# Two token transposes of a graph-attention kernel: from TensorE to block-permuted loads and VectorE

## The chip, the cores and the metric

The kernel runs on one core of one Trainium2 chip. The metric is device time in microseconds, from the start to the end of one execution. Five engines run their own instruction streams in order and meet at semaphores: TensorE (PE, with its weight loads PEld), VectorE (DVE), ScalarE (ACT), GpSimd (POOL) and SyncE (SP), which here issues every DMA.

## The reference, cut to what matters

The input x has 128 graphs of 64 nodes and 768 features. Two layers follow each other, each of the form layernorm(x + layer(x)):

```python
# layer 0: 12 heads of 64, over the neighbours that adj allows
h    = x @ W                                  # 768 x 768
attn = softmax(mask(leaky(src(tanh(h)) + dst(tanh(h)).T)))
out  = elu(attn @ h + b)
gate = sigmoid(x @ H_w.T + H_b)
x1   = layernorm(x + gate * out + (1 - gate) * x)
# layer 1: 6 heads of 128
q, k, v = x1 @ Wq, x1 @ Wk, x1 @ Wv
ctx  = softmax(mask(q @ k.T / sqrt(128))) @ v
out  = layernorm(x1 + ctx @ Wf + bf)
```

All in float32. So each token tile is multiplied from the left four times: x by W and H_w, x1 by Wv (and by Wq and Wk in layer 1). TensorE contracts over partitions, so these products need the tile with its features, not its tokens, on the partitions: x and x1 have to be transposed.

## The kernel before, in words

Two graphs make a tile of 128 tokens by 768 features (64 tiles), and two tiles make a pair (`NP` = 32 pairs). `phase_a` does layer 0 and the v product of layer 1, pair by pair; `phase_b` does the rest of layer 1 in groups of two pairs. Every product of a pair (256 tokens by 768 by 768) is done in seven half-size block products in place of eight, in Strassen's manner: class `Product` takes sums of blocks of the transposed tokens (`token_sums`, four GpSimd additions per pair, L252 to L255) and of the weights, multiplies them (L203) and puts the results together from PSUM.

**The order is written by hand.** `phase_a` fills a dictionary `events` by step with `at(step, ...)`, and `run` emits the steps in turn. A pair starts `N` = 21 steps after the one before it. At its offset `o`, pair `p` runs block `i` of the product W at step `o + i`, of G (the gate) at `o + 7 + i`; the product V (v of layer 1) of pair `p` follows at `o + 56`, thus in the steps 14 to 20 of a later pair. One step is therefore one block, and 21 blocks make one period: W, G, V of three pairs that overlap. Within a step the closures are emitted in the order in which they were registered, and each engine gets its instructions in that order.

**What a block leaves behind.** `Product.evict(i)` is called after block `i`. Blocks 0, 2 and 3 are kept as snapshots in SBUF (`snap`, ACT, L381). Blocks 1, 4 and 5 are read from PSUM and added to a snapshot by VectorE (`into`, L404 for h and the gate; L423 for v). Block 6 adds onto the PSUM tile X that blocks 0, 2 and 4 wrote, and is copied out by ACT. Four PSUM tiles go round (`psX`).

**The transposes.** `transposed(src, chunk)` makes a tile T of 128 features by 6 chunks by 128 tokens: six PE transposes against the identity into two PSUM tiles (L375), copied to SBUF by ACT (L376). `xT` calls it for x of a pair's two tiles at steps `o - 6` and `o - 5`, and `sums` runs the four GpSimd sums at `o - 4`. For x, chunk `c` of each half of 384 features holds every third feature (`chunk0`, by which the rows of W and H_w are also ordered). For x1, chunks are 128 features in a row (`chunk1`); `x1T` transposes at `o + 42` and `o + 43`, writes the result to DRAM for layer 1 (`xT_d`), and `sums` follows at `o + 44`. T tiles come from a pool of four.

**Other work of a pair.** For each of its two tiles `Tile0` runs the attention in steps after `s` (`s = o` for tile 1, `s = o + 5` for tile 0): tanh, source and target scores (L444 to L454), the exchange through DRAM of target scores (`dst_out`, `dst_in`), the exchange of halves of h in SBUF (`exchange`, `hx`), GpSimd's addition (L492), the mask on VectorE (L499), maximum, subtraction and sum (L503, L504, L511), GpSimd's scaling (L514), the transposition of probabilities on PE (L525), the aggregation (L543), elu and the mix (L562 to L583), the layernorm, and the write of x1 to DRAM (`spill`, L594).

All DMAs go through SP's single queue, in program order; an issue that waits for an engine holds those behind it.

Of the kernel before, what the change touches and what calls it, by code (L numbers as in the profile page):

```python
# [9 lines left out]
F32 = mybir.dt.float32  # L10
# [5 lines left out]
P = 128  # L16
# [45 lines left out]
def kernel(  # L62
# [31 lines left out]
    nc = tc.nc  # L94
    NB, S, D = x.shape
# [3 lines left out]
    NC = D // P  # L99
    HALF = D // 2  # L100
    CH = NC // 2
    NT = NB * S // P
    NP = NT // 2
    assert S == 64 and DH == P and E == 64 and HALF == 384 and A == 12

    x_t = x.rearrange("(t g) n d -> t (g n) d", g=2)
# [11 lines left out]
    ident = const.tile([P, P], F32, name="ident")  # L118
# [32 lines left out]
    def load15(wb, src, k):  # L151

        kb, c = divmod(k, 2)
        nc.sync.dma_start(
            wb[:, 3 * kb : 3 * kb + 3, c, :],
            src[k * P : (k + 1) * P, :].rearrange("p (n o) -> p n o", n=3),
        )

    def weight15_sum(wb, k, eng):
        to, a, b, sign = WEIGHT_SUMS[k]  # L160
        eng.tensor_tensor(wb[:, to], wb[:, a], wb[:, b], SIGN[sign])
# [7 lines left out]
    def weight_plain(wb, src, blocks):  # L169
        for kh, oh in blocks:  # L170
                nc.sync.dma_start(
                    wb[:, SLOT[kh, oh]],
                    src[kh * HALF : (kh + 1) * HALF, oh * HALF : (oh + 1) * HALF].rearrange(
                        "(c p) o -> p c o", p=P
                    ),
                )

# [71 lines left out]
    def token_sums(Ss, Ta, Tb):  # L249

        tt = nc.gpsimd.tensor_tensor
        tt(Ss[:, 0], Tb[:, :CH], Tb[:, CH:], ALU.add)  # L252
        tt(Ss[:, 1], Ss[:, 0], Ta[:, :CH], ALU.subtract)
        tt(Ss[:, 2], Ta[:, :CH], Tb[:, :CH], ALU.subtract)
        tt(Ss[:, 3], Ta[:, CH:], Ss[:, 1], ALU.subtract)  # L255
# [44 lines left out]
    def phase_a(ctx):  # L300
        k6 = ctx.enter_context(tc.tile_pool(name="k6", bufs=2))
        k3 = ctx.enter_context(tc.tile_pool(name="k3", bufs=1))
        k1 = ctx.enter_context(tc.tile_pool(name="k1", bufs=1))
        small = ctx.enter_context(tc.tile_pool(name="small", bufs=3))
        psa = ctx.enter_context(tc.tile_pool(name="psa", bufs=4, space=bass.MemoryType.PSUM))

        st = [dict() for _ in range(NP)]
# [6 lines left out]
        def load(p):  # L314
            d = st[p]
            d["x"] = []
            for i in range(2):
                t = xb[:, (2 * p + i) % 7]
                nc.sync.dma_start(t, x_t[2 * p + i])
                d["x"].append(t)  # L320
            d["adj"] = small.tile([P, 2, S], U8, name="adj")
            nc.sync.dma_start(d["adj"], adj_p[p])
# [39 lines left out]
        def chunk0(src, k):  # L362
            return src.rearrange("p (h q c) -> p h c q", h=2, c=CH)[:, k // CH, k % CH, :]

        def chunk1(src, k):
            return src[:, k * P : (k + 1) * P]

        def transposed(src, chunk):

            dst = k3.tile([P, NC, P], F32, name="T", bufs=4)  # L370
            for half in range(2):
                ps = psa.tile([P, CH, P], F32, name="pa")
                for c in range(CH):
                    k = half * CH + c
                    nc.tensor.transpose(ps[:, c, :], chunk(src, k), ident)  # L375
                nc.scalar.copy(dst[:, half * CH : (half + 1) * CH, :], ps)  # L376
            return dst

# [5 lines left out]
        def sums(d):  # L384
            Ss = k6.tile([P, 4, CH, P], F32, name="S")
            token_sums(Ss, *d["T"])
            d["S"] = Ss
# [20 lines left out]
        def start_h(d):  # L408
            d["h"] = [k3.tile([P, D], F32, name="h", bufs=3) for _ in range(2)]
            d["W"] = product(d, lambda i, c: w0_v[:, i, :, c, :], into(d["h"]))  # L410

        def start_g(d):
            d["g"] = [k3.tile([P, D], F32, name="gt", bufs=3) for _ in range(2)]
            d["G"] = product(d, lambda i, c: w1[:, i, c, :], into(d["g"]))

        def start_v(d):
            def sink(k, ps, kept):
                i, half = PLACE[k]
                o = k1.tile([P, HALF], F32, name="v", bufs=3)
                if kept is None:  # L420
                    nc.scalar.copy(o, ps)
                else:
                    nc.vector.tensor_tensor(o, ps, kept, ALU.add)  # L423
                nc.sync.dma_start(v_d[2 * d["p"] + i][:, halves(half)], o)

            d["V"] = product(d, lambda i, c: w2[:, i, c, :], sink)
# [171 lines left out]
        def at(step, *fs):  # L598
            events.setdefault(max(step, 0), []).extend(fs)

        def dense(d, key, i):
            d[key].matmuls(i)
            d[key].evict(i)
# [11 lines left out]
        for k, block in enumerate(((0, 0), (1, 0), (0, 1), (1, 1))):  # L615
            at(10 + 5 * k, lambda block=block: weight_plain(w2, Wv, [block]))
# [4 lines left out]
        for p in range(NP):  # L621
            d, o = st[p], N * p
            d["p"] = p
            if p:
                at(max(o - 20, 1), lambda p=p: load(p))

            def xT(d, i):
                d.setdefault("T", []).append(transposed(d["x"][i], chunk0))

            at(o - 6, lambda d=d: xT(d, 0))  # L630
            at(o - 5, lambda d=d: xT(d, 1))
            at(o - 4, lambda d=d: sums(d))
            at(o, lambda d=d: start_h(d))
            at(o + 7, lambda d=d: start_g(d))
            for i in range(7):
                at(o + i, lambda d=d, i=i: dense(d, "W", i))
                at(o + 7 + i, lambda d=d, i=i: dense(d, "G", i))
            for i, s in ((1, o), (0, o + 5)):
                t = Tile0(p, i)
                at(s + 6 + (i == 0), t.tanh, t.cap)  # L640
                at(s + 7, t.src_mul)
                at(s + 8, t.src_sum, t.dst_mul)
                at(s + 9, t.dst_sum, t.dst_out, t.exchange)
                at(s + 13, t.dst_in)
                at(s + 14, t.gate)
                at(s + 17, t.add)
                at(s + 18, t.mask)
                at(s + 19, t.top)
                at(s + 20, t.total)
                at(s + 23, t.probs)  # L650
                at(s + 24, t.aggregate)
                at(s + 25, t.elu)
                at(s + 26, t.mix1)
                at(s + 27, t.mix2)
                at(s + 28, t.norm1)
                at(s + 29, t.norm2)
                at(s + 30, t.spill)

            def x1T(d, i):
                if i == 0:  # L660
                    d["T"] = []
                d["T"].append(transposed(d["x"][i], chunk1))
                nc.sync.dma_start(xT_d[d["p"]][:, i], d["T"][i])

            at(o + 42, lambda d=d: x1T(d, 0))
            at(o + 43, lambda d=d: x1T(d, 1))

            def reload_T(d):
                d["T"] = []
                for i in range(2):  # L670
                    t = k3.tile([P, NC, P], F32, name="T", bufs=4)
                    nc.sync.dma_start(t, xT_d[d["p"]][:, i])
                    d["T"].append(t)

            if p != NP - 4:
                at(o + 44, lambda d=d: sums(d))

            v = o + {NP - 4: 84, NP - 2: 50, NP - 1: 45}.get(p, 56)
            if p == NP - 4:
                at(v - 7, lambda d=d: reload_T(d))  # L680
                at(v - 3, lambda d=d: sums(d))
            at(v, lambda d=d: start_v(d))
            for i in range(7):
                at(v + i, lambda d=d, i=i: dense(d, "V", i))
# [24 lines left out]
    def phase_b(ctx, wq, wk):  # L709
# [269 lines left out]
        for k in range(NC):  # L979
            at(2 + k, lambda k=k: load15(wf, Wf, k))  # L980
# [120 lines left out]
```

## Time and profile before

Median of three runs: 3027.14 us (3026.11 to 3029.84). The profiled execution spans 3023.9 us at a granted TensorE clock of 0.993.

| engine | busy us | share | instructions |
|---|---|---|---|
| PE | 2935.8 | 97% | 18852 |
| PEld | 2139.9 | 71% | 18852 |
| DVE | 1798.6 | 59% | 3531 |
| ACT | 937.8 | 31% | 1743 |
| POOL | 1640.8 | 54% | 1648 |

The DMA queue of SP moved 257.16 MB; its packets took 25.7% of the time of 16 DMA engines. Layer 0 with v takes the first half of the span, up to about 1590 us.

How to read the profile: a group line gives line, engine, operation and shapes, how often, the busy time in all, the mean of one in ns, and the idle time just before it with what ended it. A timeline line gives the start, the length and the operation, with the idle time before it in brackets. The ends of matmuls are modelled, so for PE the distance between starts says more than the lengths. L numbers are those of the kernel before.

### The profile page before, as it was taken

The numbers are of one execution on the slowest core, as the hardware profiler recorded it, in microseconds if no ns is written. First come the engines' busy times: TensorE is split into PE (matmuls) and PEld (weight loads), VectorE is DVE, ScalarE is ACT, GpSimd is POOL, SyncE is SP. The second block draws the span as 40 slices with busy tenths as digits, with TensorE's granted clock in tenths as the row PEclk, the third lists the DMA queues.
The fourth block names the chain that finished last, engine by engine and source line by source line (L and its number), as shares of the span: only waits on it lengthen the run. The fifth ranks groups of instructions, "written<-read, shape, count | busy, mean of one in ns | idle before, by whom it ended". The sixth has DMA issues, their size and how long they took to land.

```text
span 3023.9 us, 49367 instructions
## 1 busy us (share of the span) xinstructions
PE 2935.8 (97%) x18852; PEld 2139.9 (71%) x18852; DVE 1798.6 (59%) x3531; ACT 937.8 (31%) x1743; POOL 1640.8 (54%) x1648
## 2 busy tenths in 40 slices
PE   7899999999999999999899999999999999999997
PEld 4566666666666666666557888888888888888886
DVE  4666666666676666766674555555555555555556
ACT  3343443434434444444422122222112222211221
POOL 3756565665656556565574444554544455454445
PEclk9999999999999999999999999999999999999999
DMA  5232232222322222232252121222112122211221
GB/s 158 67 98 92 89 110 77 98 87 93 105 82 98 82 98 98 84 103 82 87 173 80 49 85 60 78 85 82 57 63 85 59 80 85 81 57 64 85 79 69
DMA packets 224044, 260.31 MB, mean 86 GB/s; under 512 B 91713, under 2 KB 169281, under 8 KB 223809
## 3 DMA queue, kind: packets, MB, share of 16 engines
q1 hardware_dynamic: 223808, 257.16, 25.7%
q8 instruction: 150, 2.46, 0.3%
q14 instruction: 86, 0.70, 0.1%
HBM read 143.43 MB, written 101.06 MB: 81 GB/s over the span
## 4 chain that ended last, share of the span: by engine, by line
PE 66%; POOL 16%; DVE 12%; ACT 2%; issue 2%; DMA 1%; SPq 0%; DVEq 0%; POOLq 0%
PE X L796 29%; PE X L203 29%; POOL S L766 5%; POOL Sc L778 3%; PE pa L375 2%; DVE e L573 2%; POOL xs L754 2%; POOL tmp L444 2%; PE pb L921 2%; PE pb L861 2%; POOL rstd L290 2%; DVE e L574 1%; DVE e L582 1%; DVE st L278 1%; DVE h L404 1%
## 5 line engine op out<-in xcount | busy, mean ns | idle before, releaser
L203 PE MATMUL X<-w,S 128*128 128x384 f32 x2304 | 806.2, 493 | 15.3 <-ACT snap L381 8.3
L796 PE MATMUL X<-S,w 128*128 128x256 f32 x2816 | 669.7, 383 | 18.1 <-ACT q L817 14.8
L203 PEld LDWEIGHTS X<-w,S 128*128 128x128 f32 x2304 | 425.1, 191 | 315.2 <-ACT snap L381 28.1
L203 PE MATMUL X<-w,T 128*128 128x384 f32 x1728 | 608.2, 492 | 1.8 <-ACT T L376 1.0
L796 PEld LDWEIGHTS X<-S,w 128*128 128x128 f32 x2816 | 523.7, 190 | 96.6 <-issue 20.0
L203 PEld LDWEIGHTS X<-w,T 128*128 128x128 f32 x1728 | 320.8, 192 | 201.9 <-issue 4.2
L778 POOL TENSOR_TENSOR Sc<-cT 128x256 f32<-128x256 f32 x224 | 161.4, 730 | 378.6 <-PE X L796 375.0
L796 PE MATMUL X<-w,Sc 128*128 128x256 f32 x1408 | 326.9, 383 | 3.9 <-DVE xs L839 2.6
L839 DVE TENSOR_TENSOR xs<-xs,X 128x256 f32<-128x256 f32 x512 | 208.3, 418 | 179.3 <-PE X L796 147.8
L796 PEld LDWEIGHTS X<-w,Sc 128*128 128x128 f32 x1408 | 263.4, 190 | 47.1 <-DVE xs L839 10.4
L290 POOL TENSOR_TENSOR rstd<-rstd,neg_half 128x1 f32<-128x1 f32 x126 | 69.4, 551 | 398.9 <-DVE rstd L289 398.9
L822 DVE TENSOR_TENSOR k<-k,X 128x256 f32<-128x256 f32 x320 | 133.5, 421 | 218.3 <-PE X L796 168.3
L822 DVE TENSOR_TENSOR q<-q,X 128x256 f32<-128x256 f32 x320 | 131.9, 419 | 203.5 <-PE X L796 122.4
L796 PE MATMUL X<-xb,w 128*128 128x256 f32 x960 | 236.6, 379 | 0.0
L297 ACT ACTIVATE xs<-xs,shift,rstd 128x768 f32<-128x768 f32 x62 | 63.7, 1027 | 471.9 <-POOL shift L293 467.2
L796 PEld LDWEIGHTS X<-xb,w 128*128 128x128 f32 x960 | 181.2, 190 | 24.0
L817 ACT ACTIVATE k<-X,bk_c 128x256 f32<-128x256 f32 x192 | 91.0, 474 | 304.8 <-PE X L796 304.8
L895 POOL TENSOR_TENSOR s<-s,rs 128x384 f32<-128x384 f32 x64 | 53.1, 830 | 243.4 <-DVE rs L894 220.6
L766 POOL TENSOR_TENSOR S<-xb 128x512 f32<-128x512 f32 x104 | 131.6, 1279 | 84.2 <-DMA xb<-xT_d 56.7
L514 POOL TENSOR_TENSOR s<-s,rs 128x768 f32<-128x768 f32 x64 | 94.2, 1472 | 143.9 <-DVE rs L513 134.4
L817 ACT ACTIVATE q<-X,bq_c 128x256 f32<-128x256 f32 x192 | 89.0, 470 | 258.4 <-PE X L796 258.4
L381 ACT COPY snap<-X 128x384 f32<-128x384 f32 x288 | 136.5, 479 | 82.2 <-PE X L203 79.1
(106 smaller groups left out, 4262.8 us busy)
## 6 DMA issues: line engine op xcount, KB each, us to landing
xb<-in_x_dram SPq DMA_DIRECT2D x64, 384.0 KB
s<-dst_d SPq DMA_DIRECT2D x128, 192.0 KB
x_d<-xb SPq DMA_DIRECT2D x64, 384.0 KB
xT_d<-T SPq DMA_DIRECT2D x64, 384.0 KB
v_d<-v SPq DMA_DIRECT2D x128, 192.0 KB
xb<-xT_d SPq DMA_DIRECT2D x32, 768.0 KB
xb<-v_d SPq DMA_DIRECT2D x256, 96.0 KB
xs<-x_d SPq DMA_DIRECT2D x64, 384.0 KB
```

The source lines that it names most:

```text
L203: nc.tensor.matmul(o, self.lhsT(i, c), rhs, start=first and c == 0, stop=last and c == CH - 1, skip_group_check=True,)
L290: nc.gpsimd.tensor_tensor(rstd, rstd, neg_half, ALU.pow)
L297: nc.scalar.activation(r, r, AF.Identity, bias=shift, scale=rstd)
L375: nc.tensor.transpose(ps[:, c, :], chunk(src, k), ident)
L381: nc.scalar.copy(t, ps)
L514: nc.gpsimd.tensor_tensor(self.s, self.s, self.rs[:, :, None].to_broadcast([P, A, S]), ALU.mult)
L766: eng.tensor_tensor(t, group_part(d, r0), group_part(d, r1), op)
L778: nc.gpsimd.tensor_tensor(t, pair_part(d, q, r0), pair_part(d, q, r1), op)
L796: nc.tensor.matmul(ps, self.lhsT(r, slot, c), self.rhs(r, slot, c), start=start and c == 0, stop=stop and c == 1, skip_group_check=True,)
L817: nc.scalar.activation(o[:, b], ps, AF.Identity, bias=bias[:, hd : hd + 1], scale=1.0 if positive else -1.0)
L822: nc.vector.tensor_tensor(o[:, b], o[:, b], ps, ALU.add if positive else ALU.subtract)
L839: nc.vector.tensor_tensor(o, o, ps, ALU.add if positive else ALU.subtract)
```

## The change

x and x1 are no longer transposed by PE and copied by ACT. A second load brings the tile from DRAM with its 32x32 blocks already in transposed places (`load_blocks`: eight DMAs, each 32 partitions by 4 pieces of 96 floats), into a tile `xp` of which there is one. VectorE's `transpose`, which turns each 32x32 block in itself, then gives T (`turn`, two instructions a tile). x comes from the input a second time, x1 from where `spill` put it. The purpose is to take the transposes from PE and their copies from ACT.

The first pair's x and the last pair's x1 stay on PE (`transposed`, now without its `chunk` argument). x1 now has the same order of features as x, so Wq, Wk and Wv are loaded with their rows in that order (`in_order` and `"(p c) o -> p c o"`); Wf is not. In x1's case tile 1 is turned first. The pool `small` goes from three buffers to two, which makes room for `xp`.

```diff
     def load15(wb, src, k):
         kb, c = divmod(k, 2)
+        rows = src[k * P : (k + 1) * P, :] if src is Wf else in_order(src)[k]
...
-                        "(c p) o -> p c o", p=P
+                        "(p c) o -> p c o", p=P
...
-        small = ctx.enter_context(tc.tile_pool(name="small", bufs=3))
+        small = ctx.enter_context(tc.tile_pool(name="small", bufs=2))
...
+        def load_blocks(tile_, src):
+            xp = tile_.rearrange("p (h t r) -> p h t r", h=2, t=4)
+            sv = src.rearrange("(t i) (h q r) -> q h i t r", t=4, h=2, q=4)
+            for q in range(4):
+                for h in range(2):
+                    nc.sync.dma_start(xp[q * 32 : (q + 1) * 32, h], sv[q, h])
+            return xp
+
+        def turn(xp):
+            dst = k3.tile([P, NC, P], F32, name="T", bufs=4)
+            for h in range(2):
+                nc.vector.transpose(
+                    dst[:, h * CH : (h + 1) * CH, :].rearrange("p c (t i) -> p c t i", t=4),
+                    xp[:, h].rearrange("p t (j c) -> p c t j", c=CH),
+                )
+            return dst
+
+        def blocks(src):
+            return load_blocks(k3.tile([P, D], F32, name="xp"), src)
...
+            def xb_in(d, i):
+                d.setdefault("xp", []).append(blocks(x_t[2 * d["p"] + i]))
+
             def xT(d, i):
-                d.setdefault("T", []).append(transposed(d["x"][i], chunk0))
-
-            at(o - 6, lambda d=d: xT(d, 0))
-            at(o - 5, lambda d=d: xT(d, 1))
-            at(o - 4, lambda d=d: sums(d))
+                d.setdefault("T", []).append(turn(d["xp"][i]))
+
+            if p:
+                at(o - 12, lambda d=d: xb_in(d, 0))
+                at(o - 6, lambda d=d: xT(d, 0))
+                at(o - 6, lambda d=d: xb_in(d, 1))
+                at(o - 3, lambda d=d: xT(d, 1))
+            else:
+                at(0, lambda d=d: d.update(T=[transposed(t) for t in d["x"]]))
+            at(o - 2, lambda d=d: sums(d))
...
-            at(o + 42, lambda d=d: x1T(d, 0))
-            at(o + 43, lambda d=d: x1T(d, 1))
+            if p < NP - 1:
+                at(o + 40, lambda d=d: x1_in(d, 1))
+                at(o + 42, lambda d=d: x1T(d, 1, turn(d["xp", 1])))
+                at(o + 42, lambda d=d: x1_in(d, 0))
+                at(o + 45, lambda d=d: x1T(d, 0, turn(d["xp", 0])))
+            else:
+                for i in range(2):
+                    at(o + 42 + i, lambda d=d, i=i: x1T(d, i, transposed(d["x"][i])))
...
             if p != NP - 4:
-                at(o + 44, lambda d=d: sums(d))
+                at(o + (46 if p < NP - 1 else 44), lambda d=d: x1_sums(d))
```

More of the change, by code (lines that the diff above doesn't have):

```diff
@@ L153, in load15, with in_order @@
         kb, c = divmod(k, 2)
+        rows = src[k * P : (k + 1) * P, :] if src is Wf else in_order(src)[k]
         nc.sync.dma_start(
-            wb[:, 3 * kb : 3 * kb + 3, c, :],
-            src[k * P : (k + 1) * P, :].rearrange("p (n o) -> p n o", n=3),
-        )
+            wb[:, 3 * kb : 3 * kb + 3, c, :], rows.rearrange("p (n o) -> p n o", n=3)
+        )
+    def in_order(src):
+        r = src.rearrange("(h p c) o -> h c p o", h=2, c=CH)
+        return [r[k // CH, k % CH] for k in range(NC)]
     def weight15_sum(wb, k, eng):
@@ L363, in chunk0, with transposed @@
             return src.rearrange("p (h q c) -> p h c q", h=2, c=CH)[:, k // CH, k % CH, :]
-        def chunk1(src, k):
-            return src[:, k * P : (k + 1) * P]
-        def transposed(src, chunk):
+        def load_blocks(tile_, src):
[15 more added lines that the diff above has]
+            return load_blocks(k3.tile([P, D], F32, name="xp"), src)
+        def transposed(src):
             dst = k3.tile([P, NC, P], F32, name="T", bufs=4)
@@ L373, in transposed @@
                 for c in range(CH):
-                    k = half * CH + c
-                    nc.tensor.transpose(ps[:, c, :], chunk(src, k), ident)
+                    nc.tensor.transpose(ps[:, c, :], chunk0(src, half * CH + c), ident)
                 nc.scalar.copy(dst[:, half * CH : (half + 1) * CH, :], ps)
@@ L657, in phase_a, with x1_in, x1T @@
                 at(s + 30, t.spill)
[L659 to L663, printed above, removed]
-            at(o + 42, lambda d=d: x1T(d, 0))
-            at(o + 43, lambda d=d: x1T(d, 1))
+            def x1_in(d, i):
+                d["xp", i] = blocks(x1_d[2 * d["p"] + i])
+            def x1T(d, i, t):
+                d["x1T", i] = t
+                nc.sync.dma_start(xT_d[d["p"]][:, i], t)
+            if p < NP - 1:
[6 more added lines that the diff above has]
+                    at(o + 42 + i, lambda d=d, i=i: x1T(d, i, transposed(d["x"][i])))
             def reload_T(d):
@@ L673, in reload_T, with x1_sums @@
                     d["T"].append(t)
+            def x1_sums(d):
+                d["T"] = [d["x1T", i] for i in range(2)]
+                sums(d)
             if p != NP - 4:
-                at(o + 44, lambda d=d: sums(d))
+                at(o + (46 if p < NP - 1 else 44), lambda d=d: x1_sums(d))
             v = o + {NP - 4: 84, NP - 2: 50, NP - 1: 45}.get(p, 56)
```

## The prediction

> **What bounds the kernel now.** I read the page first (busy shares, slices), then one period of the first layer, the groups by shape, and the timelines of TensorE, VectorE and the DMA queue.
>
> ```profile
> PE 2935.8 (97%) x18852; PEld 2139.9 (71%) x18852; DVE 1798.6 (59%) x3531; ACT 937.8 (31%) x1743; POOL 1640.8 (54%) x1648
> ```
> ```profile
> 599.25:646.73 47.48, 47.28 (x260) 29.00 (x259) 31.15 (x48) 19.76 (x36) 28.30 (x25) 1.00 0.28 93
> ```
> The second line is one period (21 steps, one pair of tiles) of layer 0: length, then busy PE, PEld, DVE, ACT, POOL, clock, DMA share. PE is busy 47.28 of 47.48 us, at full clock. Whatever leaves PE shortens the period, until another engine answers late. DVE has 16.3 us of idle time, and the 16 DMA engines are busy 28%.
>
> ```profile
> L376 ACT COPY T<-pa 128x384 f32<-128x384 f32 x256 | 111.1, 494 | 6.9 <-PE pa L375 6.8
> L375 PE MATMUL pa<-ident,xb 128*128 128x128 f32 x768 | 109.5, 281 | 18.1 <-ACT T L376 12.2 <-DMA xb<-in_x_dram 5.9
> ...
> L456 DVE STREAM_TRANSPOSE sdT<-sd 128x32 f32<-128x32 f32 x64 | 13.5, 212 | 2.2
> ```
> These are what the change removes, and the one place where DVE already transposes. Matmul ends are modelled, so the cost of six transpositions is read from starts:
>
> ```profile
> 631.36 2.10 PE L203 MATMUL X<-w,S 128*128 128x384 f32 x6
> 633.29 0.82 PE L375 MATMUL pa<-ident,xb 128*128 128x128 f32 x6
> 633.95 2.10 PE L203 MATMUL X<-w,T 128*128 128x384 f32 x6
> ```
> One block (a step) takes 633.29 - 631.36 = 1.93 us, six transpositions 633.95 - 633.29 = 0.66 us, with no gap around either.
>
> ```profile
> 629.68 0.56 DVE L423 TENSOR_TENSOR v<-X,snap 128x384 f32<-128x384 f32 x1 [5.53 <-PE X L203]
> 630.15 1.74 DVE L499 TENSOR_TENSOR s<-s,cap 128x768 f32<-128x768 f32 x1
> 631.82 0.54 DVE L423 TENSOR_TENSOR v<-X,snap 128x384 f32<-128x384 f32 x1
> 632.28 0.94 DVE L503 TENSOR_REDUCE mx<-s 128x12 f32<-128x768 f32 x1
> ...
> 638.74 0.56 DVE L404 TENSOR_TENSOR h<-X,snap 128x384 f32<-128x384 f32 x1 [2.23 <-PE X L203]
> ...
> 646.25 0.56 DVE L404 TENSOR_TENSOR h<-X,snap 128x384 f32<-128x384 f32 x1
> ```
> This stretch decides. DVE begins on V's block 4 as PE delivers it (629.68) and reaches W's block 4 (the last line) at 646.25. That last read matters: block 6 accumulates into the same PSUM tile X, so PE may not start it before DVE has read. In the trace block 6 starts at 647.93, 1.1 us after that read ends. Between the two reads DVE is nearly full, and the change puts three of its four transpositions here.
>
> [...] Of fp32 the trace shows only the 212 ns above. [...] the new pieces are 384 B, a size the trace lacks. [...] The trace agrees on a delay before data:
>
> ```profile
> 1887.34 0.82 SPq L268 DMA_DIRECT2D xb<-xT_d  x2
> ...
> DMA  0000000000964699999999999999899999999620
> ```
> The second line cuts 1886 to 1895 us into 40 slices: issue at 1887.34, first data in the eleventh (1888.25), 0.9 us later.
>
> **The change part by part.**
>
> *Removed from PE:* 4 x 6 transpositions a period, 4 x 0.66 = 2.64 us. Of 128 tiles 124 change (x of the first pair and x1 of the last stay): at most 124 x 0.66 = 82 us if nothing else gets in the way, 2945 us. PE's own work is then 44.8 us a period.
>
> *Removed from ACT:* 248 copies of 494 ns. ACT is busy 19.8 of 47.5 us and the snapshots PE waits for keep their place, so I count nothing.
>
> *Added to DVE:* two transpositions of 128x384 a tile. [...] So 1.16 us a tile and 4.6 us a period: 31.2 + 4.6 = 35.8 of 44.8, so DVE does not bind by its sum. The source is read with a step of three elements; [...] and I take 0.58.
>
> *Added to the DMA queue:* eight loads a tile, 32 partitions x 4 pieces of 384 B. The bytes (0.39 MB a tile, 1.57 MB on some 4.4 MB a period) fit. The issue is what counts:
>
> ```profile
> L319 SPq DMA_DIRECT2D xb<-in_x_dram x64: 327/440/1466, 2.4 to 1446.9; - x64
> L741 SPq DMA_DIRECT2D xb<-v_d x256: 512/605/1451, 1600.3 to 2976.7; - x128
> ```
> (minimum/median/maximum ns). A plain 128-row load costs 0.44 us at the median, a cut-up one of 64 x 3 pieces 0.61. I take 0.45 for 128 pieces. From first issue to use: 7 x 0.45 + 0.9 to first data + 0.85 for data and receipt = **L = 4.9 us**. Bounds: 0.36 us an issue gives 4.2, 0.61 gives 6.0. DMA engine time is no limit: 64 pieces an engine.
>
> *The new waits.* `xp` has one buffer: a load waits on the queue until DVE has turned the tile before. Two loads have spare time: x of tile 0 is issued six steps ahead, and x of tile 1 starts after the first turn (about 625.4, behind the `hx` exchange, which in the trace ends 626.65), so 627.0 + 4.9 = 631.9, just when DVE comes out of the mask. The two x1 loads have two and three steps on paper, but DVE reaches them earlier than that. In the trace's clock:
> - Turn of x tile 1: 631.9 to 633.1; V's block 5 to 633.6; maximum, subtraction, exponential, sum and reciprocal to 637.9.
> - The first x1 load issues behind the v store, 634.05, usable 638.95. DVE stands from 637.9. Of a turn's two halves the first needs seven of the loads, so the turn ends about 0.6 after the last: 639.55.
> - W's block 1 to 640.1, mask to 641.5. The second x1 load is behind the store of the first turn, issues at 640.0, usable 644.9: DVE stands 3.4 us, the turn ends 645.5.
> - Maximum 0.95, subtraction 1.4, z 1.0, sum and reciprocal 1.2, then W's block 4: read at 650.6.
>
> Queued behind DVE's two stops are the softmax and the read of block 4. PE would want block 6 at 646.5: after 629.42, where V's block 5 starts, eight blocks (15.5), one transposition of probabilities (0.65) and one aggregation (0.95, the gap in front of W's block 3 in the trace). It waits until 650.6: **4.1 us** a period.
>
> A second wait lies within that: GpSimd's four sums of x (4.7 us at 1.0 to 1.35) now start at 633.1 instead of 627.09, and the softmax scaling (1.47) behind them ends at 639.2, while PE is ready to transpose the probabilities at 637.2. These 2.0 us fall ahead of block 6, so they are part of the 4.1, and are the floor of the stall if loads were instant. SyncE's in-order queue also holds v and dst behind loads; readers of those have 5 us and more, so nothing is added.
>
> *At no cost:* the weights' row order (same transfers, same sizes), `small` with two buffers (21 steps between uses; the two per-pair lives don't overlap), x1's tile order, the final sums two steps later (V starts ten steps on).
>
> *Sum:* -2.64 + 4.1 = +1.46 us a period, times 31 = +45 us: 3027 + 45 = **3072 us**. Layer 1 reads the same transposed tiles and keeps its time.
>
> **The rivals.**
> 1. *The loads are early enough.* For it: DVE's work alone between the reads, waits on ACT included, is about 17 us against the 16.8 that PE leaves (629.68 to 646.5), and DMA engines are 72% free. Against it: one xp buffer and eight issues. With the floor of 2.0 us: 31 x (2.0 - 2.64) = -20, 3007 us. If GpSimd also gave way, up to 2945. This is the faster side.
> 2. *The queue is the bound.* Issues at 0.61 as for the 64x3 loads make L = 6.0; the two x1 loads add 2.2 us, the x load 0.5: a stall of 6.8, +4.2 x 31 = +129, 3156 us. For it: those loads are the nearest in form. Against it: they have 192 pieces rather than 128.
> 3. *DVE turns more slowly.* At 1.2 us an instruction, each turn costs 1.2 us more; two in the chain at half effect, since the first half runs during the last load, and one in full: some +2.5 us a period, 3150 us. For it: the strided read is not in the trace. [...]
> 4. *It evens out:* L = 4.2 shortens two waits by 0.7 and gives a stall of 2.7, equal to the removed work: 3027.
>
> **How the numbers follow.** Forecast 0.43; rival 1 0.22 at about 3007 and 0.07 near 2945; even 0.08; rivals 2 and 3 together 0.20. Faster 0.29, same 0.08, slower 0.63. The range runs from 2990 (rival 1 at its floor, without its 0.07 near 2945) to 3145 (most of rivals 2 and 3); left out are about 0.08 below and 0.10 above.
>
> **What would show it.** Right: periods near 48.8 us; DVE standing before the turns of x1 on the DMA, 1 and 3 us; PE waiting on DVE's h read before W's block 6; the new transposition row near 580 ns; DMA issues near 0.45 us. The step on L falls if those standing times are below 1 us in sum; the step on DVE falls if its row is far from 0.58; the whole falls if PE still shows no idle and periods of 45 us, since then block 6 does not wait for that read.

## The result, and the profile after

The changed kernel takes 3223.55 us (median of four runs, 3221.91 to 3227.63), against 3026.62 us (3025.12 to 3029.84) for the kernel before beside it: ratio 1.0651, interval 1.0633 to 1.067. It is 197 us slower; the forecast was 45 us slower. Layer 1 keeps its time: from the last read of V to the end there are 1437.5 us before and 1437.8 after. The first read of V comes at 164.0 us in place of 148.5 (+15.5). The rest, 181 us over 31 periods, is 5.9 us a period. The whole stretch between these two reads, before and after (length, busy PE, PEld, DVE, ACT, POOL, granted clock, DMA share, GB/s):

```profile
148.46:1586.36 1437.90, 1417.03 (x7713) 867.69 (x7712) 951.49 (x1388) 590.84 (x1076) 864.25 (x730) 1.00 0.29 97
164.00:1783.31 1619.31, 1415.85 (x7009) 824.63 (x7008) 1080.12 (x1623) 502.30 (x840) 842.54 (x730) 0.94 0.38 114
```

TensorE's idle time in it (length less busy time) goes from 20.9 to 203.5 us. The removed transpositions should have taken 82 us from its busy time, which falls by 1.2 us only; so the matmuls that stayed took some 81 us longer, at a granted clock of 0.94 in place of 1.00. These three, -82 + 183 + 81, are the 181 us.

The first page line of after, then one period from V's block 1 to the next, the idle stretch in it, and the stretch after that (columns as above):

```profile
PE 2933.0 (91%) x18108; PEld 2095.0 (65%) x18108; DVE 1936.8 (60%) x3779; ACT 844.7 (26%) x1495; POOL 1617.3 (50%) x1648
```
```profile
700.28:753.44 53.16, 47.66 (x236) 27.61 (x235) 35.73 (x56) 16.75 (x28) 27.58 (x25) 0.94 0.38 114
712.60:717.20 4.60, 0.03 (x1) 0.00 (x0) 2.98 (x5) 2.32 (x4) 4.15 (x5) 0.85 0.50 130
717.20:723.40 6.20, 6.15 (x60) 3.82 (x60) 2.38 (x4) 2.07 (x4) 2.38 (x2) 0.56 0.51 136
```

In the whole execution TensorE has 744 instructions fewer and is still as long busy. This period takes 53.16 us, of which 4.6 are plain idleness, and the six us after it run at 0.56 of the clock. Cut into single microseconds, the trace has the clock at 1.00 up to 715.6, about 3 us into the idle time, and at half from 716.6 to 722.6. No engine is full. The timeline of TensorE of after shows the same place:

```profile
708.60 4.03 PE L208 MATMUL X<-w,T 128*128 128x384 f32 x12
717.25 1.54 PE L549 MATMUL pa<-ident,s 128*128 128x128 f32 x6 [4.62 <-POOL s L538]
718.59 4.05 PE L208 MATMUL X<-w,S 128*128 128x384 f32 x6
723.42 4.14 PE L208 MATMUL X<-w,S 128*128 128x384 f32 x12
```

TensorE has done V's block 6 and W's block 1 and waits 4.62 us for the scaled probabilities of tile 1 (L538, which was L514 before). Then one block takes 4.05 us where it took 2.10. The timelines of VectorE, GpSimd and the DMA queue of after say why the probabilities are late:

```profile
705.00 0.56 DVE L447 TENSOR_TENSOR v<-X,snap 128x384 f32<-128x384 f32 x1 [2.94 <-PE X L208]
705.47 0.95 DVE L523 TENSOR_TENSOR s<-s,cap 128x768 f32<-128x768 f32 x1
709.14 1.28 DVE L384 STREAM_TRANSPOSE T<-xp 128x384 f32<-128x384 f32 x2 [2.72 <-DMA xp<-in_x_dram]
...
716.26 1.28 DVE L384 STREAM_TRANSPOSE T<-xp 128x384 f32<-128x384 f32 x2 [0.68 <-DMA xp<-x_d]
...
722.76 1.32 DVE L384 STREAM_TRANSPOSE T<-xp 128x384 f32<-128x384 f32 x2 [2.27 <-DMA xp<-x_d]
...
728.44 0.49 DVE L428 TENSOR_TENSOR h<-X,snap 128x384 f32<-128x384 f32 x1
```
```profile
710.57 1.00 POOL L257 TENSOR_TENSOR S<-T 128x384 f32<-128x384 f32 x1 [6.46 <-DVE T L384]
...
715.72 1.47 POOL L538 TENSOR_TENSOR s<-s,rs 128x768 f32<-128x768 f32 x1 [0.45 <-DVE rs L537]
```
```profile
704.41 3.72 SPq L377 DMA_DIRECT2D xp<-in_x_dram  x8
```

The load of x tile 1 is issued at 704.41, and VectorE, which has masked the scores of tile 1, stands 2.72 us in front of the turn (709.14 - 704.41 = 4.73 us). Behind the turn are queued V's block 5, the maximum, the subtraction, the sum; on GpSimd the four sums of x, for which it sits idle 6.46 us. Both meet in the scaling, 715.72 to 717.19. So TensorE's wait goes by GpSimd and VectorE back to a DMA, and from there to the queue: the turn of tile 0 frees the buffer `xp` at 702.06, but SP is issuing `dst`, the two `hx` and a store of v without a gap from 700.39 on, and comes to the load 2.35 us later. The two turns of x1 wait too, 0.68 and 2.27 us.

In before the same place was met just in time:

```profile
622.25 0.84 PE L375 MATMUL pa<-ident,xb 128*128 128x128 f32 x6
624.86 0.85 PE L375 MATMUL pa<-ident,xb 128*128 128x128 f32 x6
638.48 0.82 PE L525 MATMUL pa<-ident,s 128*128 128x128 f32 x6
```
```profile
636.65 1.47 POOL L514 TENSOR_TENSOR s<-s,rs 128x768 f32<-128x768 f32 x1 [3.08 <-DVE rs L513]
```

The scaling ended at 638.12 and TensorE came at 638.48. From VectorE's read of V's block 4 to the end of the scaling it is 8.44 us in before (629.68 to 638.12) and 12.19 in after (705.00 to 717.19): 2.72 of standing, 1.21 of turning, 0.58 of a longer subtraction (1.70 in place of 1.12), less 0.79 of a shorter mask (0.95 in place of 1.74). On the other side the two transposes of x1 that stood in front of the probabilities, 1.3 us, are gone. With the 0.36 us that were in hand in before, 3.75 + 1.3 - 0.36 makes 4.7 us; 4.62 are seen.

The new group on the page of after:

```profile
L384 DVE STREAM_TRANSPOSE T<-xp 128x384 f32<-128x384 f32 x248 | 161.6, 690 | 195.6 <-DMA xp<-x_d 107.6
```

690 ns is the mean of one instruction, and VectorE stood idle for 195.6 us in front of them all.

### The profile page after: what moved, and what is told of

It reads as the page before. It is cut to its first block, busy times and chain, and to the rows that moved or that the text cites. A ratio compares the mean times of both kernels' runs of the same rounds, so it can differ in the third digit from the quotient of the medians.

```text
span 3221.1 us, 49374 instructions
## 1 busy us (share of the span) xinstructions
PE 2933.0 (91%) x18108; PEld 2095.0 (65%) x18108; DVE 1936.8 (60%) x3779; ACT 844.7 (26%) x1495; POOL 1617.3 (50%) x1648
## 4 chain that ended last, share of the span: by engine, by line
PE 34%; DVE 22%; POOL 19%; SPq 12%; DMA 6%; issue 5%; ACT 1%; DVEq 0%; POOLq 0%
PE X L839 27%; SPq L377 8%; POOL S L809 5%; DMA xp<-x_d 4%; POOL tmp L468 3%; POOL Sc L821 3%; DVE e L597 3%; PE X L208 2%; DVE T L384 2%; DMA xp<-in_x_dram 2%; POOL rstd L295 2%; DVE e L598 2%; POOL xs L797 2%; DVE z L586 2%; DVE sd L478 2%
## 5 line engine op out<-in xcount | busy, mean ns | idle before, releaser
L208 PE MATMUL X<-w,S 128*128 128x384 f32 x2304 | 846.1, 515 | 33.7 <-ACT snap L405 23.4
L208 PEld LDWEIGHTS X<-w,S 128*128 128x128 f32 x2304 | 452.4, 202 | 368.4 <-ACT snap L405 43.8
L384 DVE STREAM_TRANSPOSE T<-xp 128x384 f32<-128x384 f32 x248 | 161.6, 690 | 195.6 <-DMA xp<-x_d 107.6
L549 PE MATMUL pa<-ident,s 128*128 128x128 f32 x384 | 72.7, 341 | 160.8 <-POOL s L538 160.8
L549 PEld LDWEIGHTS pa<-ident,s 128*128 128x128 f32 x384 | 56.9, 174 | 190.5 <-POOL s L538 180.5
```

The lines of the kernel that those rows point to most:

```text
L208: nc.tensor.matmul(o, self.lhsT(i, c), rhs, start=first and c == 0, stop=last and c == CH - 1, skip_group_check=True,)
L384: nc.vector.transpose(dst[:, h * CH : (h + 1) * CH, :].rearrange("p c (t i) -> p c t i", t=4), xp[:, h].rearrange("p t (j c) -> p c t j", ...
L549: nc.tensor.transpose(ps[:, jj, :], self.s[:, 2 * j : 2 * j + 2, :].rearrange("p h m -> p (h m)"), ident,)
```

## The experiments

Two theories at first. **A**: the loss is how late x tile 1 is turned, in the stretch from V's block 4 to the probabilities of tile 1, with the slow clock behind the idle time. **B** (that of the prediction): the loss is the turns of x1, by VectorE's read of W's block 4. Diffs are against the changed kernel unless another is named; each ratio is to the kernel before beside it, with its 95% interval.

### One tile kind alone

x alone by loads and VectorE:

```diff
-            if p < NP - 1:
-                at(o + 40, lambda d=d: x1_in(d, 1))
...
+            if True:
                 for i in range(2):
                     at(o + 42 + i, lambda d=d, i=i: x1T(d, i, transposed(d["x"][i])))
...
+                at(o + 44, lambda d=d: x1_sums(d))
```

> x as in the changed kernel, x1 by PE and ACT as before (with the new order of features). Theory A (the late turn of x tile 1 holds GpSimd's sums and VectorE's softmax, so PE waits 4 to 5 us for the probabilities of tile 1 and then runs at a lower clock): the wait stays, shorter by the 1.3 us that PE now spends on x1's transposes in front of it, and about 2 us of slow clock with it: a period of about 51 us, 3110 to 3160 us. Theory B (the turns of x1 and VectorE's read of W's block 4 behind them cost the time, as forecast): the cost goes, half of the removed PE work stays: about 2986 us. Theory C (traffic and issues of the loads cost it, in proportion): half of the loss, about 3125 us with no single long PE wait.

Measured: 3141.11 us, 1.0373 [1.0358, 1.0389], as A had it. TensorE waits 3.11 us for the probabilities, and the block after them takes 3.24 us.

x1 alone:

```diff
-                at(o - 6, lambda d=d: xT(d, 0))
...
+            at(o - 6, lambda d=d: xPE(d, 0))
+            at(o - 5, lambda d=d: xPE(d, 1))
+            at(o - 4, lambda d=d: sums(d))
```

> x by PE and ACT as before, x1 by loads and VectorE. Theory A: no long wait for the probabilities of tile 1 and no lowered clock; what remains is the second x1 load (two to three us of waiting on VectorE) ahead of the read of W's block 4: 3000 to 3080 us. Theory B: nearly all of the loss is here, 3150 to 3220 us. Theory C: about 3125 us.

Measured: 3214.27 us, 1.061 [1.0593, 1.0626]: here B is right, and A alone is not enough. The two losses (some 113 and 186 us) do not add up to the 197 of both. The trace of after fits this reading: the wait at the probabilities delays TensorE, and the later one is then hidden behind it. Timelines of VectorE, ScalarE and TensorE of this kernel:

```profile
714.09 1.26 DVE L384 STREAM_TRANSPOSE T<-xp 128x384 f32<-128x384 f32 x2 [4.51 <-DMA xp<-x_d]
```
```profile
717.72 0.84 ACT L531 ACTIVATE s<-s 128x768 f32<-128x768 f32 x1 [8.00 <-DVE s L528]
718.47 0.46 ACT L405 COPY snap<-X 128x384 f32<-128x384 f32 x1
```
```profile
718.98 4.21 PE L208 MATMUL X<-w,T 128*128 128x384 f32 x6 [4.88 <-ACT snap L405]
```

VectorE stands 4.51 us before the second x1 turn; maximum and subtraction come behind it; ScalarE's exponential waits 8.00 us for them; and the snapshot of W's block 3, which needs nothing of all this, is queued behind the exponential. TensorE waits for that snapshot. So B's wait exists, but it takes hold by ScalarE and one block earlier than the read that the prediction named.

### The loads taken away

What remains if no turn waits for any transfer, and what if the load is one DMA? Both kernels leave out the permutation of the blocks, so the turned tiles hold other elements; the work and its order stay.

```diff
-            return load_blocks(k3.tile([P, D], F32, name="xp"), src)
+            return src.rearrange("p (h t r) -> p h t r", h=2, t=4)
...
-                d.setdefault("xp", []).append(blocks(x_t[2 * d["p"] + i]))
+                d.setdefault("xp", []).append(blocks(d["x"][i]))
...
-                d["xp", i] = blocks(x1_d[2 * d["p"] + i])
+                d["xp", i] = blocks(d["x"][1])
```

> The changed kernel without the loads for VectorE: each turn reads a tile of x that is in SBUF anyway (for x the tile itself, for x1 the pair's tile 1), so the output holds other elements in those places; the permutation and 31 x 4 x 8 DMA issues are left out, the turns stay where they are and wait for no transfer. This is the floor of my forecast: 2.0 us of stall in a period at the probabilities of tile 1, 3007 us. Theory A now (with one plain load, which took 3.7 us from issue to use, the kernel took 3123, a wait of 1.4 us before the turn of x tile 1 left): that wait goes too, 1.3 to 2.0 us in a period with what the clock gives back, 3050 to 3085 us, since the turns themselves and the removed transpositions keep the probabilities late by about 1.5 us. Rival (loads were all of it): 2990 to 3010. Rival (turns alone keep it slow, and the loads cost only what one load fewer showed): 3110 or more.

```diff
-            for q in range(4):
-                for h in range(2):
-                    nc.sync.dma_start(xp[q * 32 : (q + 1) * 32, h], sv[q, h])
+            nc.sync.dma_start(tile_, src)
```

> The changed kernel with one plain load of the tile (128 rows of 3072 bytes) in place of the eight of a block each: this leaves out the permutation of the blocks, so the turned tiles hold other elements, with the same turns, order, buffer and waits. The time from first issue to use falls from 4.7 us to about 2.2. Theory A (the loss is how late the turn of x tile 1 ends): its wait of 2.7 us is nearly gone, the wait for the probabilities falls from 4.6 to about 2.1 us, and so does the slow clock behind it: 31 x (2.5 + 2.7) less, 3050 to 3110 us. Rival (the loss is VectorE's own time for the turns in that stretch, and the loads are a small part): 3150 us or more. If the loads were all of it: 3000 us or less.

Measured: without loads 3043.41 us, 1.0045 [1.0028, 1.0062]; with one load 3123.41 us, 1.0315 [1.0299, 1.033]; with eight 3223.55. Both came out beside what A expected, by 7 us below and 13 us above, and neither rival did. The plain load was expected to take 2.2 us from issue to use and took 3.72 (issued 714.24, turned 717.96); seven further issues of 0.46 us add only 1.0 us. While they go out in after (704.41 to 708.13) the DMA engines are 56% busy; what share of that is these loads' data was not separated. TensorE at the probabilities, with one load and with none, and the granted clock of the stretch behind them in each:

```profile
725.81 1.54 PE L547 MATMUL pa<-ident,s 128*128 128x128 f32 x6 [3.06 <-POOL s L536]
727.14 4.05 PE L208 MATMUL X<-w,S 128*128 128x384 f32 x6
```
```profile
725.81:732.19 6.38, 6.38 (x61) 4.02 (x61) 3.95 (x5) 2.07 (x4) 4.51 (x5) 0.54 0.86 302
```
```profile
647.38 0.87 PE L549 MATMUL pa<-ident,s 128*128 128x128 f32 x6 [1.80 <-POOL s L538]
648.09 2.10 PE L208 MATMUL X<-w,S 128*128 128x384 f32 x6
```
```profile
647.38:651.01 3.63, 3.63 (x60) 2.49 (x60) 1.34 (x2) 1.97 (x4) 2.33 (x2) 1.00 0.90 317
```

From the probabilities to the block after the aggregation there are 6.38 us after a wait of 3.06, and 3.63 us after a wait of 1.80. Of these two waits, which differ by 1.26 us, the longer costs 2.75 us more behind it. So without any wait for a load 180 of the 197 us are gone: that the loads come late is what makes the change slow. This run takes the traffic away with the waits; but the third of the moved kernels below has all the loads, and takes only 13 us more than the kernel before, so the traffic is not the cause. Even so nothing is gained: 48.0 us a period in place of 47.48, although TensorE has 2.64 us less to do.

### The clock

24 transpositions of the identity, written to PSUM and overwritten, keep TensorE busy in front of the probabilities, in the changed kernel and in the kernel with x alone:

```diff
+                    if self.i == 1 and q == 0:
+                        for k in range(24):
+                            nc.tensor.transpose(ps[:, k % CH, :], ident, ident)
```

> The changed kernel with 24 PE transposes of the identity (about 2.6 us, results overwritten) in front of the transposes of the probabilities of tile 1, in PE's idle time. If the lowered clock after the wait comes from the length of the idle time (theory A): the idle time falls from 4.6 to about 2 us, the clock stays at 1.0, some 2.7 us a period come back: about 3140 us. If the clock is lowered by anything else: 3223 us as without them, or more.

> The kernel with x alone changed (one wait of 3.1 us a period, for the probabilities of tile 1), with 24 PE transposes of the identity (2.7 us, results overwritten) in that wait. If the lowered clock follows from the length of PE's idle time: the wait falls to under 1 us, the slow blocks after it (1.8 us more than at full clock) run at full speed: about 3085 us against 3141. If the clock falls for another reason: 3141 us or more.

Measured: 3258.39 us, 1.0767 [1.0749, 1.0785], and 3144.29 us, 1.039 [1.0374, 1.0405]: no gain, both expectations missed. At the place of the dummies the clock did what they said. In the first, 2.04 us of idleness remain before the probabilities and the next block takes 2.10 us again. TensorE then waits at W's block 5, as in the kernel with x1 alone, and there the clock falls again: the mean granted clock of the whole run rises only from 0.964 to 0.974. Waits of TensorE from 200 to 1500 us (us in total, times, longest):

```profile
PE X L208 <- ACT snap L405: 81.0, 30, 4.7
PE pa L552 <- POOL s L538: 48.6, 24, 3.4
```

In the second the block takes 2.10 us in place of 3.24 and the mean clock rises from 0.977 to 0.989, but the dummies themselves wait 1.70 us for a PSUM tile and end 1.35 us after the probabilities were ready (739.00 against 737.65), which takes back most of what the clock gives. That with less idleness the clock stays up is shown at these two places (2.10 us a block in place of 4.05 and 3.24); what the time would be with the clock alone repaired is not, since no run took its fall away without moving a wait.

### Loads earlier, turns where they were

Two buffers `xp` (`tmp` shares the place of `z` to make room), and loads issued ahead:

```diff
+            return load_blocks(k3.tile([P, D], F32, name="xp", bufs=2), src)
...
+                self.tmp = k3.tile([P, D], F32, name="z")
...
+                at(o - 12, lambda d=d: xb_in(d, 1))
...
+                at(o + 37, lambda d=d: x1_in(d, 1))
...
+                at(o + 40, lambda d=d: x1_in(d, 0))
```

> Two buffers of xp (room from tmp sharing z's place), every load issued at least five steps ahead of its turn; turns and sums at the changed kernel's steps. Theory A: VectorE no longer stops on the DMA; the turn of x tile 1 ends about 2.7 us earlier, GpSimd's sums and the scaling with it; PE waits about 2 us for the probabilities, the clock stays at 1.0, the period is about 46.8 us: about 3005 us, below the kernel before. Theory B: also faster, but PE's wait would be at W's block 6. Theory C (same traffic, same issues): no faster than 3200 us.

Measured: 3126.33 us, 1.0322 [1.0307, 1.0338], far from the 3005 that A gave. VectorE no longer stands before a turn, but 16 issues in a row hold the scores of the `dst` exchange back on the same queue, GpSimd's addition waits for them (3.90 us in the period shown by its timeline), the mask is late, and TensorE still waits 4.26 us for the probabilities. The wait changed its cause and stayed. So this run does not show what earlier loads alone are worth; the one without loads does.

### Turns moved

Loads early, x turned 6 and 5 steps ahead of W, both x1 turns after the softmax, at `o + 50` ahead of the block 1 of a gate:

```diff
+                at(o - 8, lambda d=d: xb_in(d, 1))
...
+                at(o - 5, lambda d=d: xT(d, 1))
...
+                t = o + (44 if p == NP - 2 else 50)
...
+                at(t, lambda d=d: x1T(d, 1, turn(d["xp", 1])))
+                at(t, lambda d=d: x1T(d, 0, turn(d["xp", 0])))
```

> All turns moved out of the stretch between V's block 5 and W's block 5: both of x straight after V's block 1 (sums one step later), both of x1 in the gap before G's block 1 (six steps later), two buffers of xp, loads issued ahead and behind the dst exchange. Theory A2 (what costs is anything put on VectorE or GpSimd between V's block 5 and W's block 5, a chain of softmax steps that TensorE already met just in time, plus the lowered clock after a wait of over 3 us): the stretch shrinks to about 16.3 us from 22.97, waits stay near 1 us, the clock at 1.0, a period of about 46.3 us: 2970 to 3000 us. Theory D (VectorE's 5.3 us of added work cost their time wherever they stand): 3150 us or more. Theory C (traffic and issues of the loads): no less than 3120 us.

Then the mask of tile 1 a step earlier; then, in place of that, all of tile 1's softmax a step or more earlier and GpSimd's gate additions later:

```diff
+                at(s + 17 + (i == 0), t.mask)
```

> As the kernel with the turns moved, and the mask of tile 1 one step earlier, before the read of V's block 4, in the idle time that the removed transposes leave. Theory A2: the softmax chain of tile 1 ends about 1 us earlier and takes most of the wait for the probabilities: 10 to 30 us below the kernel with the turns moved. Theory D: no change.

```diff
+                e = i == 1
+                at(s + (14 if e else 17), t.add)
+                at(s + 18 - e, t.mask)
+                at(s + 19 - e, t.top)
+                at(s + 20 - e, t.total)
...
+                at(s + (23 if e else 18), t.gate)
```

> The kernel with both x and x1 moved (3070 us) with the same earlier softmax of tile 1. Theory A: 10 to 40 us less, 3030 to 3060, with the wait of the input product for the gate's subtraction left (1.3 to 1.8 us in a period). Rival (bound by V's block 5): within 6 us of 3070.

Measured: 3070.22 us, 1.0136 [1.0118, 1.0153]; 3074.17, 1.0156 [1.0141, 1.0171]; 3041.98, 1.0045 [1.003, 1.006]. The first missed what was expected by 70 us, though its rivals lie further off, the second missed too, and the third came out as expected. The move returns 153 of the 197 us, the softmax order 28 more, the mask alone nothing. In the first of them TensorE waits about equally in two places (200 to 1500 us); the earlier softmax takes the first away, and the second stays (longest 2.6 us):

```profile
PE pa L549 <- POOL s L538: 46.8, 27, 2.1
PE X L208 <- DVE gt L428: 45.4, 26, 1.8
```

The second is VectorE's read of the gate: the turns stand before work that the gate needs. VectorE is 77% busy (459.65 of 600 us), so it is not its sum that fails; TensorE's waits lie in two stretches in which its answers are due.

x1 alone, with its turns at `o + 47` and `o + 50` and the sums at `o + 51` (diff against x1 alone):

```diff
+                t = o + (42 if p == NP - 2 else 47)
...
+                at(t, lambda d=d: x1T(d, 1, turn(d["xp", 1])))
+                at(t, lambda d=d: x1_in(d, 0))
+                at(t + 3, lambda d=d: x1T(d, 0, turn(d["xp", 0])))
```

> The kernel with x1 alone changed, its two turns moved from the steps where W begins to five and eight steps later, behind the softmax of tile 0 and W's blocks; same loads, same work. Theory A2: from 3214 us to under the kernel before, 2985 to 3020 us. Theories C and D: 3150 to 3214 us.

Measured: 3113.04 us, 1.0285 [1.0258, 1.0312]; 101 us better than unmoved, and 93 above the end of what was expected. TensorE now waits 2.2 us in a period for VectorE's read of the gate. No run found a place for x1's turns that costs nothing.

### x alone, moved

The kernel with x alone, with the two buffers and the x steps of the moved kernel (loads at `o - 12` and `o - 8`, turns at `o - 6` and `o - 5`, sums at `o - 4`):

> x alone comes by DRAM and VectorE (x1 stays on TensorE), with two xp buffers, its loads 12 and 8 steps before the stage, its turns 6 and 5 steps before and the sums 4 before, that is, ahead of the stretch in which the softmax of tile 1 is made. Theory A (the loss is the time at which the turn of x tile 1 ends, in the stretch from V's block 4 to the probabilities of tile 1): nothing waits for the turn any more, the removed transpositions give up to 31 x 1.33 = 41 us, less what VectorE's two turns delay elsewhere: 2985 to 3015 us. Rival (VectorE has no room for the turns anywhere, each is paid for by TensorE): 3050 us or more. The experiment with x alone, unmoved, took 3141.

The same with the softmax order shown above:

> As the run before it, and the softmax of tile 1 (mask, maximum, sum) is put one to two steps earlier, GpSimd's addition of the gate one step later. Theory A: the wait for the probabilities of tile 1 (2.1 us in a period in the experiment with everything moved) falls by 0.5 to 1.5 us, so 10 to 40 us less than the run before it. Rival (the softmax chain is bound by what it starts from, V's block 5, and not by its place in the order): within 6 us of the run before it.

And, without that order, with pair 1's x left on TensorE too:

```diff
+            if p == 1:
+                for i in range(2):
+                    at(o - 6 + i, lambda d=d, i=i: d.setdefault("T", []).append(transposed(d["x"][i])))
```

> The experiment with x moved ahead (3019 us), with pair 1's x left on TensorE too, so that no load for VectorE waits behind the exchanges of the first pair. There the first read of V's block 1 came 9.9 us later than in the kernel before (158.3 to 148.5 us). Theory: these 9.9 us are the cost of the first loads behind the queue, and return: 3008 to 3013 us. Rival (the start is slow for another reason): within 3 us of 3019.

Measured: 3019.29 us, 0.9968 [0.9957, 0.998]; 3169.45, 1.0467 [1.0449, 1.0484]; 3012.53, 0.9948 [0.9932, 0.9965]. The first ended 4 us above what was expected, the third within it. Both are faster than the kernel before, clear of their intervals but by 0.3 and 0.5% only. Periods are 46.0 to 47.3 us: at best the whole 1.33 us of two removed transposes are gained, mostly 0.2 to 0.4. The third takes 6.8 us less than the first, of the 9.9 us by which the first was later at V's first read.

The softmax order that gained 28 us above loses 150 here, against what I expected. ScalarE and TensorE of that kernel:

```profile
699.31 0.84 ACT L579 ACTIVATE gt<-gt 128x768 f32<-128x768 f32 x1 [4.75 <-POOL gt L578]
701.07 0.84 ACT L579 ACTIVATE gt<-gt 128x768 f32<-128x768 f32 x1 [0.92 <-POOL gt L578]
701.82 0.46 ACT L405 COPY snap<-X 128x384 f32<-128x384 f32 x1
```
```profile
702.33 3.86 PE L208 MATMUL X<-w,S 128*128 128x384 f32 x6 [3.41 <-ACT snap L405]
```

The gate's activations wait on ScalarE for GpSimd's late additions, and the snapshot that TensorE needs is queued behind them; 3.41 us, and the slow clock again.

## Why the prediction was wrong

The direction was right, the size was not. The forecast was -2.64 + 4.1 = +1.46 us a period; the period shown is 5.68 us longer than before (53.16 - 47.48). Its parts: -2.64 removed; +4.62 idle at the probabilities; +0.71 at one snapshot; +2.54 slow clock (6.17 us from the probabilities to the next block pair, 717.25 to 723.42, against 3.63 in the kernel without loads). That is 5.2; 0.5 is left over.

**Two steps failed.** The stall was priced by its idle time alone, with nothing for the clock behind it; and it was put in the wrong place, since x tile 1 was taken to arrive just in time. Over all periods the forecast had 127 us of stall and none of slow clock. The runs have 183 us more of idle time, 81 of slower matmuls and 15.5 at the start: the clock is 81 of the 152 us that the forecast fell short, the longer waits 56. That 4.1 us a period came so near to the 4.62 measured is luck, as they are waits at different places.

- **Removed work, -2.64 us.** Held: blocks at full clock keep their pace (1.93 us from start to start in before and in after, 704.73 to 706.66), and without loads the period of 47.97 us is 44.84 + 1.80 + 1.04 at two snapshots, but for 0.3.
- **VectorE's instruction, 0.58 us.** It took 0.69, so 1.3 us a turn in place of 1.16. The 0.58 was the author's estimate, which the trace of before does not show: its only transposition by VectorE, of 128x32, took 0.21 us. It was 16% short; the rival of 1.2 us fell.
- **L = 4.9 us.** 4.73, 4.85 and 4.64 for the three loads that are waited for in the period shown, with 0.46 us an issue. The 0.85 us in it for data and receipt was the author's estimate: from the end of the last issue to use the forecast had 1.3 us, and the first of the three took 1.01 (708.13 to 709.14). The queue rival (6.0) fell, though single loads do take that long: 6.54 us for one load of x in after (1185.25 to 1191.79).
- **VectorE stands 1.05 and 3.4 us before x1's turns.** 0.68 and 2.27.
- **x tile 1 arrives just in time.** It does not: VectorE stands 2.72 us. The times of V's block 4 and of the mask were read from the trace of before, but x's own two transposes (622.25 and 624.86) lay between V's blocks 1 and 4: block 4 now follows 4.72 us after block 1 (705.00 - 700.28) and not 6.06. The mask takes 0.95 us in place of 1.74, so VectorE comes out of it another 0.79 earlier. And the load starts 4.13 us after block 1 where the forecast had 3.4, as the exchanges end 0.33 later and a store of v is issued ahead of it. The three make 2.9, less 0.17 by which L was too long: 2.7. About half of the wait is thus the removed work itself, which had covered the load; why the mask is faster no run shows. Had this step held, the loss would still have been there: with x left on TensorE the change cost 186 us, by the turns of x1.
- **The floor of 2.0 us at the probabilities is part of the 4.1.** The floor itself was right: without loads 1.80 us. But the wait of the step above comes on top of it and makes 4.62, and so TensorE's main wait is here and not at W's block 6.
- **W's block 6 waits for VectorE's read of W's block 4 (4.1 us).** It does not: in the trace of after the read ends at 728.93, and block 6 starts at 729.74 with no wait. TensorE had lost its time by then. With x on TensorE a wait of 4.88 us does appear, one block earlier and by ScalarE's queue: the snapshot of block 3 behind the exponential. The forecast counted nothing for ScalarE, as it had work taken away.
- **The clock was missing from the sum.** 2.54 us in the period shown, 81 us over all, by itself more than the forecast's loss: the forecast had a stall of 4.1 us and priced only the stall. The traces show 0.54 to 0.56 of the clock behind waits of 3.06 and 4.62 us, and 1.00 behind 1.80. A wait of 2.10 us lowered it too in the first of the moved kernels, where the next block took 3.41 us in place of 2.10 (more in the last section).
- **The start.** 15.5 us went before the first read of V, which the sum by periods did not have.
- **The rival with early loads** (3007 us) fell as well: with no loads at all 3043. Its stall was right; two snapshots and a start 5.4 us later (153.8 us) were not in it.

The wait in after is one chain: V's block 1, the issues for the exchanges and its store on SP's queue, the load, the turn, softmax, GpSimd's scaling, the probabilities, TensorE. TensorE was nearly full before, yet in this stretch the others were only just in time for it; making it faster there made it wait.

## What to carry to other kernels

Before pricing removed work on the busy engine, find which late answers that work was covering, and move the others' due times forward by what is removed. Price a stall of TensorE with what the clock adds behind it (here 2.75 us behind a wait of 3.06, 2.54 behind 4.62), and look at everything queued on the in-order engines behind a waiting instruction, small copies for TensorE above all (with x1 alone a snapshot behind the exponential made TensorE wait 4.88 us). Work moved to an idle-looking engine belongs where nothing near is due: the x turns at their first place cost 113 us. With a second buffer, and with load and turn of tile 1 and the sums two steps earlier, they gained 10, and 17 with pair 1 left on TensorE.

## What the runs showed of the hardware

- TensorE's clock after a wait: after 1.80 and 2.04 us the next block took its usual 2.10 us; after 2.10 us in the first of the moved kernels it took 3.41 us, after 3.11 us 3.24, after 3.06 and 4.62 us 4.05. One wait alone tells little. Counted over layer 0 of all sixteen traces, the 6.2 us behind a wait of TensorE had a mean clock under 0.95 in 5 of 65 cases for waits of 1 to 1.75 us, in 14 of 150 for 1.75 to 2.0, in 30 of 64 for 2.0 to 2.75, in 111 of 129 for 2.75 to 4, and in all 92 above 4. After alone has 0 of 13, 0 of 1, 2 of 4, 3 of 4 and 33 of 33 of these.
- VectorE's 32x32 transposition of 128x384 float32 took 0.69 us in the mean in after (0.64 to 0.81). A turn of two took 1.28 us behind a wait of 2.72 us for its load and 1.34 us without a wait (the turn of tile 0 at 700.72); without loads single ones took 0.66 to 0.69 us.
- A plain load of 0.39 MB took 3.72 us from issue to use in the period shown, eight cut-up ones in its place 4.73; the median of the 32 loads of x that were waited for in after is 4.85.
- VectorE's subtraction over 768 columns took 0.96 to 2.64 us in the moved kernel. In after it took 1.70 us while one of GpSimd's sums beside it took 1.72 in place of 1.00. Why both were longer there no run separated.
